# Two images' rows first: the end of a mixture-of-experts layer in another order, on one core of Trainium2

## The chip, the core and the metric

The kernel runs on one core of a Trainium2 chip. The metric is the device time of one execution in microseconds (us), less is better; "before" and "after" are medians of several executions. The core has five engines that run side by side, each with its own instruction queue: TensorE (PE; its weight loads are PEld), VectorE (DVE), ScalarE (ACT), GpSimd (POOL) and SyncE (SP). Data move between the on-chip memory and DRAM by DMA, which SP, ACT and POOL issue from their queues. An engine runs its queue strictly in order: what stands behind a waiting instruction waits too.

## What is computed

Input are 4 images of 256 channels on 32 x 32 points, so 4 x 1024 tokens. A first layer (a selective scan, convolutions, attention over all tokens of an image, a depthwise convolution) makes `x`. Then follows the part that the change is about, a layer of 8 experts of which each token uses two:

```python
t = tokens(x)                                   # (4, 1024, 256)
xf = layernorm(t).reshape(-1, 256)
top_w, top_i = top_k(xf @ Wg + bg, 2)           # two experts of each token
top_w = softmax(top_w)
for e in range(8):
    h = gelu(xf @ W1[e] + b1[e])                # 256 -> 1024
    out += w_dense[:, e:e+1] * (h @ W2[e] + b2[e])   # 1024 -> 256
x = channels_first(t + out)                     # (4, 256, 32, 32)
```

## The kernel before

**Two parallel streams.** The kernel writes out the order of every engine by hand (`tc.manual_schedule`): generators for the scan, the convolutions, the attention, the routing and the expert tiles each give a few instructions and then a number of ticks to wait, and `beat()` lets whichever is due go on. While the last image is still in the first layer, the expert tiles of earlier images fill TensorE.

**Routing.** When an image is ready, `dispatch` writes its tokens, as rows of 256, to the DRAM table `Y` (the residual `t`), finds the two experts of each, and scatters the normalised rows to the DRAM table `XS`, where every expert has a region of its own, filled in the order of the images. So an expert's first rows belong to images 0 and 1, its last ones to image 3.

**Tiles and series.** The expert products are made in tiles of 256 rows of one expert (in some of 320, the "wide" series, which take a short rest along). Which expert and which rows a tile has is known only on the chip; the program has a fixed number of places for tiles, in four series: `SERIES = (8, 8, 21, 8)`. Series 0 and 1 run on the rows of the images that are already there. Series 2 (called `rest`) and 3 (`wide`) share out all that is left after image 3. Of these the last 9 and the last 4 places are "late": they are rarely needed, and stand behind a branch on the chip (`tc.If(any_late > 0)`). For each series, `table` and its callers `series` and `wide_series` compute with some 20 small DVE instructions which expert each place has and its first row; SP reads these numbers from the chip's memory into registers before it issues the loads of a tile.

**The order of the tiles** is the list `order` in `tiles()`: the 16 of series 0 and 1, then four times one wide tile and three of `rest`, 32 in all. I number them 0 to 31. A tile has these steps, with their lines in the profile:

- `rows` (L2164): SP loads the rows, `xs<-XS`; `load` (L2198 to L2203): SP loads the expert's weights, `w`, 2 MB in four transfers, and its biases, `b`. Both are written out while the tile before runs; weights have two sets of buffers, so a transfer waits until the tile before last is done with its set.
- `front` (L2222 to L2246): TensorE transposes the rows into `xp`, DVE copies them to `xT` and reads each row's weight and destination. It stands in TensorE's order in the middle of the second product of the tile before.
- `tile`: the first product `h<-xT,w` on TensorE (L2263), GELU on ACT to `hs` (L2268), the second product `y<-w,hs` (L2276), the bias on DVE to `ys` (L2290, both blocks of 128 rows at once), the row weights on DVE (L2295), and for each block one indirect DMA that POOL issues and that adds the rows to `Y` (L2303). Adds of one tile wait for the adds of the tile before.

**The end.** After the last tile a few instructions judge whether the sums of the attention's exponentials stayed in range (`any`, `bad`, L1608 and L1609; if not, the whole network would be run again in another form). Then `run` branches over the late tiles, and `bring_back` runs for each of the four images: SP reads the image's rows from `Y` in two transfers of 512 KB (`yy<-Y`, L2319; all eight stand at the head of the work behind the branch), TensorE transposes them (`op`, L2328), DVE and ACT copy them (`o`, L2334 and L2332), and ACT writes each half, 512 KB, to the output (L2335). `o` has two buffers.

**The branch.** Every engine runs it for itself. Where it is not taken, each engine passes a short block that adds to the semaphores what the skipped work would have added; it first waits until the semaphores have reached the count that they have before the branch. SP does this for the eight semaphores of the DMAs that SP and ACT issue, POOL for those of its own DMAs.

Of the kernel before, what the change touches and what calls it, by code (L numbers as in the profile page):

```python
# [14 lines left out]
P = 128  # L15
C = 256
# [32 lines left out]
LATE, LATE_WIDE = 9, 4  # L49

# [25 lines left out]
def network(  # L76
# [71 lines left out]
    with tc.tile_pool(name="w_conv", bufs=1) as wp, tc.tile_pool(  # L148
# [239 lines left out]
        def a8(name):  # L388
            return act8.tile([P, NC2, N], F32, tag="a8", name=name)
# [7 lines left out]
        def a4(name):  # L397
            return act4.tile([P, N], F32, tag="a4", name=name)
# [979 lines left out]

        def tiles():
# [5 lines left out]
            between = (experts.SERIES[rest] - LATE) // some  # L1385
            for i in range(some):
                order.append((wide, i))
                order += [(rest, i * between + k) for k in range(between)]
# [50 lines left out]
            def ahead(n, at):  # L1439

                if experts.placed and wide not in tables:
                    tables[wide] = experts.series(wide, temp)
                    tables[rest] = experts.series(rest, temp)
                if n == len(order):
                    return
                if n in got and len(got[n]) > 4:
                    return
                if n in xs and n in got and at >= 5:
                    front(n)
                    return  # L1450

                if known(n) and n not in tables_of:
                    table(n)
                if n not in xs and sent(n):
                    rows(n)
                if n not in got and known(n):
                    load(n)

            for n in range(len(order)):
# [19 lines left out]
                for at, _ in enumerate(experts.tile(  # L1479
                    n, s, got[n], hs,  # L1480
                    act4.tile([P, len(experts.blocks(s)), C], F32, tag="a4", name=f"ys_{n}"),
                )):
                    if at < 4:
                        loaded[0] = None
                    ahead(n + 1, at)
                    yield T.get(("pace",), 1)
# [54 lines left out]
        with tc.manual_schedule(engines=ALL):  # L1541
# [54 lines left out]
            start(one_by_one(joined(B - 1), around(B - 1), sent_off(B - 1)))  # L1596
            drain()

    if not shifted:
        with tc.tile_pool(name="judge", bufs=1) as jp:  # L1600
            most = jp.tile([P, 1], F32, name="most")
            for i, span in enumerate((SPAN, INVERSE)):
                nc.vector.tensor_scalar(sums[:, i, :], sums[:, i, :], span, None, ALU.is_lt)
            nc.vector.tensor_reduce(most, sums.rearrange("p a b -> p (a b)"), AX.X, ALU.min)

            nc.vector.tensor_scalar(most, most, 1.0, None, ALU.is_lt)
            any_ = ps_tile("any")
            nc.tensor.matmul(any_[0:1, 0:1], ones_mean[:, 0:1], most, start=True, stop=True)  # L1608
            nc.vector.tensor_scalar(bad, any_[0:1, 0:1], 0.0, None, ALU.is_gt)  # L1609

    experts.run(experts.tables)
# [11 lines left out]
class Experts:  # L1623
# [19 lines left out]
    def __init__(self, ctx, tc, psum, B, b1, ident, eps5, ones_mean, Wg, bg, W1, W2, b2, out):  # L1643
# [74 lines left out]
        self.read = []  # L1718
        self.apart = m0.tile([P, 1], F32, name="apart")
# [251 lines left out]
    def count_up(self, s, temp):  # L1971

        nc, K, n = self.nc, self.NTOK // self.T, self.SERIES[s]
        steps = temp(f"steps_{s}", [P, NE, K])
        base = {self.WIDE: 0, self.WIDE - 1: REST}.get(s, self.T - 1)
        nc.gpsimd.iota(
            steps, [[0, NE], [self.T, K]], base=base,
            channel_multiplier=0, allow_small_or_imprecise_dtypes=True,
        )
        which = temp(f"which_{s}", [P, n, NE])  # L1980
        nc.gpsimd.iota(
            which, [[1, n], [0, NE]], base=0, channel_multiplier=0,
            allow_small_or_imprecise_dtypes=True,
        )
        self.numbers[s] = steps, which

# [8 lines left out]
    def table(self, temp, keep, name, n, ntile, which, done=None):  # L1995
# [3 lines left out]
        ends = keep(f"ends_{name}", [P, 1, NE])  # L1999
        nc.vector.tensor_tensor_scan(  # L2000
            ends[:, 0, :], self.every[:, 0:NE], ntile[:, 0, :], 0.0, ALU.mult, ALU.add
        )
        starts = temp(f"starts_{name}", [P, 1, NE])
        nc.vector.tensor_tensor(starts, ends, ntile, ALU.subtract)
        S = [P, n, NE]
# [7 lines left out]
        nc.vector.tensor_scalar(expert, expert, float(NE - 1), None, ALU.min)  # L2013
# [7 lines left out]
        nc.vector.tensor_tensor(which, which, self.region[:, 0:1, :].to_broadcast(S), ALU.add)  # L2021
# [13 lines left out]
    def use(self, s, ends):  # L2035

        late = LATE_WIDE if s == self.WIDE else LATE
        over = self.used[s] = self.m0.tile([P, 1], mybir.dt.int32, name=f"over_{s}")
        self.nc.vector.tensor_scalar(
            over, ends[:, :, NE - 1 : NE].rearrange("p a e -> p (a e)"),  # L2040
            float(late - self.SERIES[s]), 0.0, ALU.add, ALU.max,
        )

    def wide_series(self, temp):
# [34 lines left out]
        self.use(s, ends)  # L2079
        return table  # L2080

    def series(self, s, temp):
# [7 lines left out]
        if s == self.WIDE - 1:  # L2090
            assert before + n == self.NTILE
            table, _, ends = self.table(temp, self.kept, s, n, self.left, which, self.done)
            self.use(s, ends)
            self.any_late = self.m0.tile([P, 1], mybir.dt.int32, name="any_late")
            nc.vector.tensor_tensor(
                self.any_late, self.used[s], self.used[self.WIDE], ALU.add
            )
            return table
# [18 lines left out]
    def run(self, tables):  # L2117

        tc, nc = self.tc, self.nc
        with tc.tile_pool(name="moe2", bufs=2) as m2:  # L2120
            def load(v):
                return nc.values_load(
                    v[0:1, 0:1], min_val=0, max_val=sum(self.SERIES),
                    skip_runtime_bounds_check_because="made from counts of at most NTOK rows",
                )

            def late_tile(s, i):
                j, W = f"{s}_{i}", self.width(s)
                w1 = m2.tile([P, NC2, DFF], F32, tag="w1", name=f"w1_{j}")
                w2 = m2.tile([P, NHC, C], F32, tag="w2", name=f"w2_{j}")  # L2130
                got = self.load(
                    s, i, tables[s], [w1], [w2], m2.tile([P, C], F32, tag="b2", name=f"b2_{j}")
                )
                xs = m2.tile([P, len(self.blocks(s)), self.ROW], F32, tag="xs", name=f"xs_{j}")
                self.rows(s, i, tables[s], xs)
                got += self.front(
                    j, s, i, tables[s], xs, m2.tile([P, NC2, W], F32, tag="xT", name=f"xT_{j}")
                )
                for _ in self.tile(
                    j, s, got, [m2.tile([P, NHC, W], F32, tag="hs", name=f"hs_{j}")],  # L2140
                    m2.tile([P, len(self.blocks(s)), C], F32, tag="ys", name=f"ys_{j}"),
                ):
                    pass

            with tc.If(load(self.any_late) > 0):
                for s, late in ((self.WIDE - 1, LATE), (self.WIDE, LATE_WIDE)):
                    n = self.SERIES[s]
                    with tc.If(load(self.used[s]) > 0):
                        for i in range(n - late, n):
                            late_tile(s, i)  # L2150
            for b in range(self.B):
                self.bring_back(b, m2)
# [96 lines left out]
    def tile(self, j, s, got, hs, ys):  # L2249
# [9 lines left out]
        for k0 in range(0, NHC, each):  # L2259
# [9 lines left out]
            if k0 % 2 == 0:  # L2269
                yield  # L2270
        for t, n in blocks:
            if t % 2 == 0:
# [9 lines left out]
            if parts > 1:  # L2282
# [3 lines left out]
                nc.vector.tensor_tensor(ys[0:n, t], yp[0:n, 0:C], other, ALU.add)  # L2286
            elif t % 2 or t == len(blocks) - 1:
# [6 lines left out]
        for t, n in blocks:  # L2294
            nc.vector.tensor_scalar(  # L2295
                ys[0:n, t, :], ys[0:n, t, :], wgt[0:n, t, :], None, ALU.mult
            )

        added = []
        for t, n in blocks:  # L2300
            if t:
                nc.gpsimd.memset(self.apart, 0.0)
            ins = nc.gpsimd.indirect_dma_start(  # L2303
                out=self.Y[:, :],
                out_offset=bass.IndirectOffsetOnAxis(ap=dest[0:n, t, :], axis=0),
                in_=ys[0:n, t, :], in_offset=None, compute_op=ALU.add,
            )
            for other in added:
                self.tc.declare_no_dep(ins.ins, other.ins, reason="no two share a row")
            self.follow(ins, self.added, "a row may be added to by both")  # L2310
            added.append(ins)
        self.added = added

    def bring_back(self, b, m2):

        nc, NT = self.nc, self.NT
        y = m2.tile([P, NT, C], F32, tag="yy", name=f"yy_{b}", bufs=self.B)
        for h in range(2):
            nc.sync.dma_start(  # L2319
# [3 lines left out]
        o = m2.tile([P, NC2, N], F32, tag="o", name=f"o_{b}")  # L2323
# [112 lines left out]
```

## Time and profile before

| | us |
|---|---|
| median of 3 runs | 2177.85 (2172.67 to 2179.22) |
| the profiled execution | 2175.2 |
| its span, first to last instruction | 2173.3 |
| TensorE busy | 1937.3 (89% of the span) |
| DVE busy | 1536.4 (71%) |
| ACT busy | 1211.4 (56%) |
| POOL busy | 1042.7 (48%) |
| granted TensorE clock, mean | 0.956 |
| data moved by DMA | 251.41 MB, 116 GB/s in the mean |

The profile is of one execution. Lines of the timeline give the start and the length in us, the engine, the line of the program, the operation with its tiles as output<-input, its shape, and in brackets how long the engine had been idle and what released it. SPq, ACTq and POOLq are the queues of these engines: a row DMA_DIRECT2D there is the issue of a transfer, not its duration. Lines of a source query give the count and the shortest, median and longest duration in ns, and the first and last start in us. The tables by stage give for each engine its busy time and the number of its instructions, then the granted clock of TensorE (1.00 is full speed), the busy share of the 16 DMA engines and what they moved.

### The profile page before, as it was taken

The page shows a single profiled execution, that of the slowest core. Times are in us where ns is not written, and L with a number is a line of the kernel's source. Part 1 is how long each engine was busy: PE and PEld are TensorE (multiplying, and loading weights), DVE is VectorE, ACT ScalarE, POOL GpSimd, SP SyncE. Part 2 cuts the span into 40 slices and gives each one's busy share as a digit, 9 for nine tenths or more (in the row PEclk, how much of TensorE's full clock was granted, in tenths as well). Part 3 has the DMA queues.
Part 4 walks back from the last instruction along what each step waited for, and adds up shares of the span by engine and source line. Part 5 has one row for each costly group of instructions (what it writes and reads, how often), then busy time and mean ns, then how long its engine had stood idle before and what let it go on. Part 6 is the DMA issues. An engine that isn't in the chain of part 4 may idle for free. (4 is left out here: it accounts for less than half of the span.)

```text
span 2173.3 us, 28179 instructions
## 1 busy us (share of the span) xinstructions
PE 1937.3 (89%) x8690; PEld 867.6 (40%) x8690; DVE 1536.4 (71%) x2231; ACT 1211.4 (56%) x2272; POOL 1042.7 (48%) x930
## 2 busy tenths in 40 slices
PE   6778778999987999988789999679999999999995
PEld 2112112322212332222124223126743668888884
DVE  4989999957998989699898998985364445121111
ACT  4665657668777577776566876524277423222221
POOL 0887887712788850476887026742021113322221
PEclk8888999999999999998999999889999999999997
DMA  3565553401444431154634204344330267866665
GB/s 104 148 156 131 127 123 93 100 28 57 104 117 114 105 73 40 29 138 104 168 81 118 69 22 107 85 164 139 92 82 21 55 189 215 255 182 187 178 159 167
DMA packets 157088, 251.41 MB, mean 116 GB/s; under 512 B 34740, under 2 KB 101332, under 8 KB 156664
## 3 DMA queue, kind: packets, MB, share of 16 engines
q1 hardware_dynamic: 136560, 223.47, 37.6%
q0 software_dynamic: 12720, 17.32, 4.1%
q10 hardware_dynamic: 7640, 8.65, 1.2%
q8 instruction: 72, 1.18, 0.2%
q14 instruction: 96, 0.79, 0.1%
HBM read 137.22 MB, written 36.62 MB: 80 GB/s over the span
## 5 line engine op out<-in xcount | busy, mean ns | idle before, releaser
L744 POOL TENSOR_TENSOR dA<-hs,cs 128x512 f32<-128x512 f32 x512 | 682.0, 1340 | 376.1 <-DVE hs L736 307.6
L715 ACT ACTIVATE dA<-dts,A 128x512 f32<-128x512 f32 x512 | 358.9, 718 | 160.9 <-DMA dts<-dt 66.7
L754 PE MATMUL yp<-dA,quads 128*32 128x512 f32 x1024 | 289.0, 637 | 87.8 <-POOL dA L744 76.0
L2303 POOL DMA_INDIRECT Y<-ys,dest x68 | 109.5, 1610 | 429.6 <-DVE ys L2295 422.5
L1133 ACT ACTIVATE e<-st 128x512 f32<-128x512 f32 x512 | 263.8, 606 | 89.4 <-PE st L1123 88.9
L2268 ACT ACTIVATE hs<-h,b 128x256 f32<-128x256 f32 (+1 forms) x256 | 110.0, 478 | 345.7 <-PE h L2263 233.8
L725 DVE TENSOR_TENSOR dBu<-dts,bs 128x512 f32<-128x512 f32 x384 | 259.6, 677 | 47.4 <-PE bs L707 13.4
L736 DVE TENSOR_TENSOR_SCAN hs<-dA,last,dBu 128x512 f32<-128x512 f32 x192 | 243.6, 1269 | 1.8 <-PE yp L754 1.1
L2276 PE MATMUL y<-w,hs 128*128 128x256 f32 (+1 forms) x1088 | 242.6, 382 | 0.5 <-ACT hs L2268 0.3
L2263 PE MATMUL h<-xT,w 128*128 128x256 f32 (+1 forms) x1024 | 239.6, 390 | 1.1 <-DVE xT L2226 1.1
L736 DVE TENSOR_TENSOR_SCAN hs<-dA,dBu 128x512 f32<-128x512 f32 x192 | 231.6, 1206 | 1.0 <-PE var L435 0.7
L1180 DVE TENSOR_TENSOR e<-e,e 128x512 f32<-128x512 f32 x256 | 168.2, 718 | 77.8 <-ACT e L1133 47.8
L2263 PEld LDWEIGHTS h<-xT,w 128*128 128x128 f32 x1024 | 195.2, 192 | 42.8 <-issue 8.6
L2276 PEld LDWEIGHTS y<-w,hs 128*128 128x128 f32 (+1 forms) x1088 | 197.1, 188 | 37.7 <-issue 10.1
L2226 DVE COPY xT<-xp 128x512 f32<-128x512 f32 (+1 forms) x36 | 23.3, 646 | 250.9 <-PE xp L2222 245.1
L707 PE MATMUL bs<-u,xpwT_s 128*32 128x512 f32 x1024 | 161.2, 660 | 41.3 <-DVE hs L736 18.0
L1123 PE MATMUL st<-qk 32*128 32x512 f32 x1024 | 174.0, 638 | 0.3
L754 PEld LDWEIGHTS yp<-dA,quads 128*32 128x32 f32 x1024 | 50.5, 113 | 303.4 <-POOL dA L744 198.6
L1172 PE MATMUL av<-e,v 128*32 128x512 f32 x1024 | 139.5, 604 | 0.0
L1936 POOL DMA_INDIRECT XS<-XR,to x64 | 65.4, 1021 | 90.3 <-ACT e L1133 53.9
L1123 PEld LDWEIGHTS st<-qk 32*128 32x128 f32 x1024 | 59.5, 183 | 115.3 <-issue 85.6
L1144 PE MATMUL av<-e,every 128*32 128x512 f32 x512 | 85.2, 596 | 2.7 <-DVE e L1180 2.6
(335 smaller groups left out, 2639.1 us busy)
## 6 DMA issues: line engine op xcount, KB each, us to landing
dts<-dt SPq DMA_DIRECT2D x512, 128.0 KB
w<-in_W_dram SPq DMA_DIRECT2D x124, 512.0 KB
cs<-cd SPq DMA_DIRECT2D x512, 64.0 KB
xs<-XS SPq DMA_DIRECT2D x32, 260.0 KB
xd<-xn SPq DMA_DIRECT2D x64, 128.0 KB
xn<-in_x_dram SPq DMA_DIRECT2D x8, 512.0 KB
XL<-xl SPq DMA_DIRECT2D x8, 512.0 KB
xl<-XL SPq DMA_DIRECT2D x4, 1024.0 KB
```

The costliest lines, as they stand in the source:

```text
L707: nc.tensor.matmul(bs[r], xpwT_s[:, n, s : s + 1].to_broadcast([P, 32]), T[b, n, "u"][:, half(h)], start=True, stop=True,)
L715: nc.scalar.activation(dA, T[b, n, h, "dts", g][:, 0, :], AF.Exp, scale=A[:, g, n, q : q + 1])
L725: nc.vector.tensor_tensor(dBu, T[b, n, h, "dts", g][:, 1, :], T[b, n, h, "bs", q], ALU.mult)
L736: nc.vector.tensor_tensor_scan(hs, T[b, n, h, "dA", i], dBu, 0.0 if h == 0 else last, ALU.mult, ALU.add)
L744: nc.gpsimd.tensor_tensor(dA, hs, T[b, n, h, "cs", q], ALU.mult)
L754: nc.tensor.matmul(T[b, n, h, "yp"][ts(g, 32)], quads, T[b, n, h, "dA", q * GD + g], start=False, stop=(q == GS - 1),)
L1123: nc.tensor.matmul(sts[i], k[r, ts(kt, P)], q[r, half(h)], start=True, stop=not shifted)
L1133: ins = nc.scalar.activation(es[i], sts[i], AF.Exp, scale=1.0 / HD**0.5)
L1172: nc.tensor.matmul(accs[0][ts(i, HD)], v8[:, kt, ts(4 * g + i, HD)], es[i], start=(kt == 0), stop=(kt == NK - 1),)
L1180: nc.vector.tensor_tensor(first[i], first[i], es[i], ALU.add)
L2263: nc.tensor.matmul(hp[:, i, :], w1(c, k0 + i), xT[:, c, :], start=(c == 0), stop=(c == NC2 - 1))
L2276: nc.tensor.matmul(yp[ts(k % parts, n), ts(t % 2, C)], hidden(k)[:, ds(t * P, n)], w2(k), start=(k < parts), stop=(k >= NHC - parts),)
```

## The change

In the order of the tiles, the first wide tile is followed by eight tiles of `rest` (`EARLY = 8`), then by one more, and then wide ones and `rest` ones alternate: W, 8 R, R, W, R, W, R, W, R. The table of `rest` is sorted anew: places go first to those tiles of each expert that still hold rows of images 0 and 1 (`SOON = 2`), expert by expert, then to the others, so it is computed for 16 kinds instead of 8. It is computed when the first wide tile runs; before, both tables were computed as soon as image 3 had been placed. Should the tiles with rows of images 0 and 1 be more than eight, or should a wide tile hold such rows, `redo` is set and these two images are read and turned once more in the branch.

`bring_back` is split into `fetch` (the reads) and `turn` (transposes, copies, writes). The reads of images 0 and 1 are written out in tile 26, the first tile behind the nine of `rest`; they are turned directly behind the last tile, ahead of the branch. Images 2 and 3 are read and turned behind it. The last tile has its two blocks of rows in two banks, and adds the first block's rows while the second block's product runs. The judging of the sums is a generator of its own that runs while later tiles do. The late tiles use the pools of the main part instead of a pool of their own.

```diff
+EARLY, SOON = 8, 2
...
             some = experts.SERIES[wide] - LATE_WIDE
-            between = (experts.SERIES[rest] - LATE) // some
+            order += [(wide, 0)] + [(rest, i) for i in range(EARLY)]
+            final = len(order)
+            between = (experts.SERIES[rest] - LATE - EARLY) // some
             for i in range(some):
-                order.append((wide, i))
-                order += [(rest, i * between + k) for k in range(between)]
+                order += [(wide, i)] * (i > 0)
+                order += [(rest, EARLY + i * between + k) for k in range(between)]
...
                 if experts.placed and wide not in tables:
                     tables[wide] = experts.series(wide, temp)
+                if wide in tables and rest not in tables and order[n - 1] == (wide, 0):
                     tables[rest] = experts.series(rest, temp)
...
                     ahead(n + 1, at)
+                    if n == final + 1 and at == 4:
+                        for b in range(SOON):
+                            experts.fetch(b, a8(f"yy_{b}"))
                     yield T.get(("pace",), 1)
...
             start(one_by_one(joined(B - 1), around(B - 1), sent_off(B - 1)))
+            if not shifted:
+                start(judged())
             drain()
-    if not shifted:
...
-    experts.run(experts.tables)
+            for b in range(SOON):
+                experts.turn(b, a8(f"o_{b}"))
+
+        experts.run(experts.tables, a8, a4, a2)
...
+            first, second = both[:, :, 0:NE], both[:, :, NE : 2 * NE]
+            nc.vector.tensor_tensor(first, self.soon, self.done, ALU.subtract)
+            nc.vector.tensor_scalar(first, first, 0.0, None, ALU.max)
+            nc.vector.tensor_tensor(first, first, self.left, ALU.min)
+            nc.vector.tensor_tensor(second, self.left, first, ALU.subtract)
...
+            table, _, ends = self.table(temp, self.kept, s, n, both, which, done, 2 * NE)
...
+            with tc.If(load(self.redo) > 0):
+                for b in range(SOON):
+                    self.fetch(b, a8(f"yy_{b}_again"))
+                    self.turn(b, a8(f"o_{b}_again"))
+        for b in range(SOON, self.B):
+            self.fetch(b, a8(f"yy_{b}"))
+        for b in range(SOON, self.B):
+            self.turn(b, a8(f"o_{b}"))
...
+            elif apart:
+                nc.vector.tensor_tensor(ys[:, t], yp[:, ts(t % 2, C)], b2_s, ALU.add)
+                weigh(t, n)
+                add(t, n)
```

## The prediction

> **What bounds the kernel now.** I read the page's busy shares first, then busy time by stages, then the timeline of the end, then the two places that the change touches earlier. The page's chain of waits names only the last 0.6%, so the end is followed by the timeline instead. By stages (engine columns PE, PEld, DVE, ACT, POOL, then granted clock, DMA share, GB/s):
>
> ```profile
> 1870.00:2135.00 265.00, 265.00 (x1251) 222.27 (x1249) 50.39 (x168) 62.17 (x141) 61.78 (x59) 1.00 0.63 170
> 2135.00:2174.00 39.00, 12.06 (x68) 10.34 (x66) 6.68 (x12) 4.68 (x8) 3.23 (x3) 0.64 0.68 226
> ```
>
> From 1870 to 2135 TensorE is never idle: it alone sets when the last product ends, and DMA has 37% of its time free. After it come 38 us in which TensorE works 12. That end, line by line:
>
> ```profile
> 2128.15 7.07 PE L2276 MATMUL y<-w,hs 128*128 128x256 f32 x32
> ...
> 2138.47 1.56 POOL L2303 DMA_INDIRECT Y<-ys,dest  x1 [0.19 <-POOLq L2145]
> 2143.75 7.93 SPq L2319 DMA_DIRECT2D yy<-Y  x8
> ...
> 2148.49 4.75 PE L2328 MATMUL op<-ident,yy 128*128 128x128 f32 x24 [13.16 <-DMA yy<-Y]
> ...
> 2151.13 0.45 ACTq L2335 DMA_DIRECT2D out_dram<-o  x1
> ...
> 2165.91 0.38 ACTq L2335 DMA_DIRECT2D out_dram<-o  x1
> ```
>
> Call X the end of the last product, 2128.15 + 7.07 = 2135.22. The last add is issued at X + 3.25, the eight reads of Y start at X + 8.5, the last write is issued at X + 30.7, the span ends at X + 38.1. Between the last add and the reads lies the branch's skipped side:
>
> ```profile
> L2145 POOLq EVENT_SEMAPHORE  x6: 17/30/43, 2138.3 to 2142.3; - x6
> ...
> L2145 POOLq INC_SWDGE_SEM  x1: 986/986/986, 2142.4 to 2142.4; - x1
> ```
>
> So the add has landed by 2142.3 (3.8 us after its issue), POOL needs 0.99 us more, then SP may read. From there DMA is the limit: 4.19 MB are read and 4.19 MB written, and the DMA view of this window shows 350 to 400 GB/s nearly throughout. A 512 KB transfer takes about 1.4 us at 370 GB/s.
>
> **The change, part by part.**
>
> *Order of tiles, and the inputs.* I took the routing from the reference on the given inputs. Before the last series experts 0 to 5 have had 3, 3, 2, 3, 3, 2 tiles; 12 normal and 4 wide tiles are left, as many as are laid out; 6 tiles (at most 8 fit) still hold rows of images 0 and 1, and no wide one does. So neither the late tiles nor the repeat run. The same 32 tiles run, 14.3 us for a normal and 18.1 us for a wide one in this stage, in another order: 0.
>
> *Judging the sums.* A one-column product (2 records, 0.19 us at 2135.15) and a compare of 0.13 us leave the end; they land in tile 5, near 1730, where TensorE has gaps (44.8 of 50 us busy). +0.1 on the path.
>
> *Table of the last series.* Before, it is built right behind the wide one, ahead of tile 13's copy. Afterwards it is built when the first wide tile (tile 16) has begun, twice as wide, and SP can't load tile 17's rows and weights before it is there:
>
> ```profile
> 1840.61 0.16 DVE L2000 TENSOR_TENSOR_SCAN ends<-every,left 128x8 f32<-128x8 f32 x1
> ...
> 1844.36 0.18 DVE L2027 TENSOR_SCALAR table<-first 128x21 int32<-128x21 f32 x1
> ...
> 1845.45 7.17 PE L2263 MATMUL h<-xT,w 128*128 128x256 f32 x32 [0.28 <-DVE xT L2226]
> ...
> 1891.00 0.62 DVE L2295 TENSOR_SCALAR ys<-ys,wgt 128x256 f32<-128x256 f32 x2
> ...
> 1902.14 0.60 PE L2222 MATMUL xp<-ident,xs 128*128 128x128 f32 x4
> ```
>
> First the gain: the 3.9 us of DVE at 1840.6 shrink to eight small operations (some 1.8 us), and TensorE's 0.28 us behind them go: -0.3. Then the cost: in DVE's order the new table stands behind tile 15's weighing, over at 1891.62. It is the old chain of 3.9 us, plus 0.17 us for each of nine operations on 336 instead of 168 columns, one more region add (0.4), and eight small ones (0.2 each): about 7.9 us, so 1899.5. SP takes 0.65 us to the issue of the next rows (in SP's timeline: b's issue over at 1910.2, xs at 1910.85), a transfer's data begin 1.2 us after issue, 260 KB take 0.7, and landing is known 1.3 us after the last byte (in the DMA view the last write's data are through at about 2169.8, the wait for it is over at 2171.2). Rows are there at 1903.4 to 1904; TensorE wants them at 1901.93, when the first weight load for this transpose starts (SP had issued them at 1877.91). In between nothing else is queued for it, so it waits 1.7 us. Bounds: 0 if the table is quicker, 4 if DVE's dependent steps or SP are slower; 1.7 is built from rows nearest to it. Weights follow the rows: 2 MB issued by 1904 land by 1910 for products at 1909.7 (w1 first, by 1907): covered. POOL's wider iotas (0.98 us for 168 columns at 1798.7) lie where POOL is 3/4 idle.
>
> *Reading images 0 and 1 beside later tiles.* Four 512 KB reads stand on SP behind tile 27's loads and ahead of tile 28's. They wait for tile 25's adds, about 7 us into tile 26 (an add is issued 3.3 us after a tile's end and lands 3.8 later). While SP waits, tile 28's rows and weights stand behind it: SP is past at 11 us and data at 15 us into tile 26; the rows are needed at 18.1 + 10.8 = 29 us and the weights at 32. Slack of 12 us: cost 0, as DMA is 37% free. Tile 26's adds must wait until the reads are over, but are not ready before 19 us. Without this cover every further us of SP's wait would be one of TensorE's.
>
> *The last tile in two halves.* The second half's sum (0.42 as for 64x256, half of 0.69 else) and weighing (0.31) precede one add, issued at X + 0.95 instead of X + 3.25. Alone it would let the reads start at X + 6.2.
>
> *Turning images 0 and 1 behind the last product.* 32 transposes at 0.133 (8 in 1.06) are 4.3 us of an idle TensorE. Writes are issued at X + 1.75, 2.9, 4.0, 5.0; data begin 1 us after the first, 4 x 1.4 us: X + 8.4, known at X + 9.7.
>
> *The new wait.* SP's skipped side of the branch waits for all eight hardware-DMA semaphores to reach their counts before it adds to them. Before, no such transfer was open there. In the built order of the changed kernel the four writes of images 0 and 1 count up four of these. So SP can't read images 2 and 3 at X + 6.2, but at about F = X + 10.0. Queued behind it: all four remaining reads, hence everything.
>
> *Reads, turning and writing of images 2 and 3.* Data F + 1.7 (2143.75 to 2145.4) to F + 7.4; the last half is known at F + 8.7; its turning and copies take 2.7 (2148.46 to 2151.13): write issued F + 11.4. ACT issues the second write behind a copy of the next image, so four writes end at F + 14.5, known 15.8, end 2.1 later: F + 17.9.
>
> Here the clock weighs against the change. The row: in this end TensorE ran 24 transposes in 4.75 us (0.198 each), cold at first and then faster. [...] The turning is now two bursts with 10 us between. If all of the second stayed cold, a half would take 2.1 us against an arrival each 1.4, and the last write would be issued 2.4 us later. By the row it keeps up; I take the row, and keep 2.4 for the range.
>
> **The sum.** X moves by +0.1 - 0.3 + 1.7 = +1.5. The end moves from X + 38.1 to X + 27.9: -10.2. Together -8.7 us, on the profiled execution's 2175.2 us (span 2173.3): 2166.5. The median of the three runs, 2177.85, lies 2.65 above that execution; with the same difference 2169.1.
>
> **The rivals.**
> *A: the writes don't hold the reads.* Then F = X + 6.2 and reads overlap the first writes; some 0.5 us is lost to sharing: X + 24.6, with X + 1.5: -12, 2165.9. For it: semaphores may have been met by then if writes are quick. Against: four writes can't be done before X + 8.
> *B: the same, but dearer.* Table stall 4, cold transposes 2.4, or writes beside the adds at 300 GB/s (+1.3 on F): -3 to -6, within what counts as no change; about 2173.
> *C: slower.* SP's wait in front of the reads of Y, in tile 26, starves tiles 28 and later. Price: 1 us of TensorE per us beyond 12 us of slack; it must exceed 12 + 8.7 = 21 us to cost more than the end gains, and 27 us to be seen; at 30 us the result is about 2187. Against: tile 25's adds are the only thing waited for, and adds landed within 4 us of issue here.
> *D: the change doesn't do what it says*, since a tile too many makes the branch be taken and images 0 and 1 be read and turned again: by the counts above (6 of 8) it isn't; it would add some 20 us. Counted with C.
>
> **Chances.** Forecast 60%, A 15%, B 20%, C with D 5%. A measurement of this kernel can tell about 0.3% (6.5 us) from no change; the forecast's gain is 8.7, so with runs that differ by 6 us some of it falls inside. Faster by over 0.3%: 0.85 x 60 + 15 + 0.2 x 20 = 70%; within: 9 + 16 = 25%; slower 5%. Range 2163 to 2174.5: from A less 3 us of scatter to B's dear end.
>
> **What would show it.** Tile 17's rows are issued on SP near 1900 and TensorE idles 1 to 3 us before that transpose. Reads of Y appear inside tile 26 with TensorE still full to the end. After X: an ACT write within 2 us, the first read of images 2 and 3 about 10 us after X and just behind the fourth write's landing, the end 28 us after X. I am wrong if the reads begin 6 us after X (A), if TensorE is idle in tiles 27 to 29 (C), or if line groups of late tiles appear (D).

## The result and the profile after

The median goes from 2176.07 us (12 executions, 2171.6 to 2180.85) to 2168.16 us (12 executions, 2163.2 to 2174.57): ratio 0.9967, 95% interval 0.9957 to 0.9978, so 4.8 to 9.4 us less. 2169.1 was forecast. The profiled execution after the change took 2167.03 us with a span of 2165.3.

The stages again, with the same columns as before the change (engines, granted clock, DMA share, GB/s), cut at the end of the last product:

```profile
1870.00:2136.50 266.50, 266.50 (x1257) 223.41 (x1256) 58.17 (x199) 61.92 (x140) 63.55 (x61) 1.00 0.65 178
2136.50:2166.00 29.50, 9.34 (x65) 8.83 (x63) 6.12 (x10) 4.68 (x8) 1.57 (x1) 0.77 0.68 228
```

TensorE is still never idle up to the last product; the stretch behind it is 29 us instead of 38. The timeline of the changed end:

```profile
2129.59 7.07 PE L2365 MATMUL y<-w,hs 128*128 128x256 f32 x32
...
2136.49 3.66 PE L2412 MATMUL op<-ident,yy 128*128 128x128 f32 x32
2137.79 1.57 POOL L2350 DMA_INDIRECT Y<-ys,dest  x1 [1.77 <-DVE ys L2343]
2138.24 0.39 ACTq L2419 DMA_DIRECT2D out_dram<-o  x1
...
2141.36 0.61 ACTq L2419 DMA_DIRECT2D out_dram<-o  x1
2147.55 2.08 SPq L2399 DMA_DIRECT2D yy<-Y  x4
2151.49 5.69 PE L2412 MATMUL op<-ident,yy 128*128 128x128 f32 x32 [11.34 <-DMA yy<-Y]
2152.67 0.69 DVE L2418 COPY o<-op 128x512 f32<-128x512 f32 x1 [12.23 <-PE op L2412]
...
2157.99 0.38 ACTq L2419 DMA_DIRECT2D out_dram<-o  x1
```

X is now 2129.59 + 7.07 = 2136.66. Images 0 and 1 are turned at once, their four writes are issued at X + 1.6 to X + 4.7, and SP starts the four remaining reads at F = X + 10.9. The last write is issued at X + 21.3, the span ends at X + 28.6. Why F is so late stands on the line of the branch (count, shortest, median and longest ns, first and last start):

```profile
L2208 POOLq EVENT_SEMAPHORE  x6: 17/30/43, 2138.6 to 2144.0; - x6
L2208 SPq EVENT_SEMAPHORE  x4: 17/17/17, 2141.7 to 2147.2; - x4
...
L2208 PEldq COMPARE_BRANCH  x1: 4871/4871/4871, 2138.6 to 2138.6; - x1
...
L2208 POOLq INC_SWDGE_SEM  x1: 986/986/986, 2144.1 to 2144.1; - x1
```

POOL is through with the last add at 2144.1 + 0.99 = 2145.1; SP's skipped side only gets through its semaphores at 2147.2, and 0.35 us later come the reads. The four rows of SPq are its waits for the four writes. The trace's DMA records have the bulk of the writes' data until 2145.9 (X + 9.2) and their last packets until 2146.9.

Images 0 and 1 are read in tile 26, which begins at 2038.56 (issues in SP's queue):

```profile
2045.91 2.03 SPq L2399 DMA_DIRECT2D yy<-Y  x4
...
2048.57 0.38 SPq L2233 DMA_DIRECT2D xs<-XS  x1
```

SP is past them 10 us into the tile. At the wait for the new table, TensorE's weight load is held by 0.41 us, while its products run on without a gap:

```profile
1899.64 0.18 DVE L2061 TENSOR_SCALAR table<-first 128x21 int32<-128x21 f32 x1
...
1900.77 0.39 SPq L2233 DMA_DIRECT2D xs<-XS  x1
...
1903.51 0.42 PEld L2291 LDWEIGHTS xp<-ident,xs 128*128 128x128 f32 x4 [0.41 <-DMA xs<-XS]
```

### The profile page after: what moved, and what is told of

Read it like the earlier page. It is cut to its first block, busy times and chain, and to the rows that moved or that the text cites. A ratio compares the mean times of both kernels' runs of the same rounds, so it can differ in the third digit from the quotient of the medians.

```text
span 2165.3 us, 28187 instructions
## 1 busy us (share of the span) xinstructions
PE 1931.0 (89%) x8690; PEld 867.6 (40%) x8690; DVE 1540.5 (71%) x2252; ACT 1212.3 (56%) x2272; POOL 1043.4 (48%) x931
## 5 line engine op out<-in xcount | busy, mean ns | idle before, releaser
L728 DVE TENSOR_TENSOR dBu<-dts,bs 128x512 f32<-128x512 f32 x384 | 259.6, 677 | 46.0 <-PE bs L710 10.8
L710 PE MATMUL bs<-u,xpwT_s 128*32 128x512 f32 x1024 | 162.9, 669 | 40.3 <-DVE hs L739 17.3
```

Source lines behind the costliest of these rows:

```text
L710: nc.tensor.matmul(bs[r], xpwT_s[:, n, s : s + 1].to_broadcast([P, 32]), T[b, n, "u"][:, half(h)], start=True, stop=True,)
L728: nc.vector.tensor_tensor(dBu, T[b, n, h, "dts", g][:, 1, :], T[b, n, h, "bs", q], ALU.mult)
```

## The experiments

My theory was the one on record: the early reads and the early turning shorten the end, and the price is that SP's skipped side of the branch waits for the early writes. The main rival was A: these writes hold nothing. All numbers of the end are counted from X, since X itself drifts (second experiment). F and the end are read in the one profile of each kernel (of the kernel before there are two). The measured ends, in us:

| kernel | F - X | end - F | end - X |
|---|---|---|---|
| before | 8.5 | 29.6 | 38.1 |
| before, profiled again | 8.7 | 30.2 | 38.8 |
| halves of the last tile alone | 6.4 | 30.0 | 36.4 |
| four output buffers alone | 8.6 | 28.1 | 36.6 |
| changed, no early reads | 6.1 | 27.4 | 33.6 |
| changed, turned behind the branch | 6.3 | 22.7 | 29.0 |
| changed | 10.9 | 17.7 | 28.6 |
| changed, early writes left out | 7.0 | 19.8 | 26.8 |
| changed, two early writes | 8.5 | 21.1 | 29.5 |
| changed, last tile undivided | 12.8 | 18.5 | 31.3 |
| changed, TensorE kept busy | 10.8 | 18.0 | 28.8 |
| changed, all ahead of the branch | 6.5 | 23.9 | 30.4 |
| changed, reads in tile 26 four times | 11.2 | 18.2 | 29.3 |
| changed, slow table | 10.9 | 17.3 | 28.2 |

The last two rows change something ahead of the end and nothing in it. So the same end came at X + 28.2, X + 28.6 and X + 29.3 in three profiles: where two rows differ by about 1 us or less, no effect is shown.

**Do the early writes hold the reads?**

```diff
-                experts.turn(b, a8(f"o_{b}"))
+                experts.turn(b, a8(f"o_{b}"), False)
...
-            nc.scalar.dma_start(
+            if write:
+                nc.scalar.dma_start(
```

> The changed kernel without the four early writes: images 0 and 1 are read and turned as there, but not written, so these two images of the output are left out. X is the end of the last product, F the start of the reads of images 2 and 3; the changed kernel had F = X + 10.9 and its span ended at X + 28.6. My theory (SP's skipped side of the branch waits for the landing of those writes): the add is issued at X + 1.1, lands 3.8 later as in the kernel before, POOL needs 1.0, so F = X + 6.2 and the end about F + 17.8 = X + 24. Rival 1 (the writes hold nothing, SP needs that time anyway): F stays at X + 10.9. Rival 2 (the add itself takes 6.2 us to land in this place, whether writes run or not): F = X + 8.5.

F fell to X + 7.0. What SP waited for shows it directly (engine and line, releaser, us in total, times, longest). The changed kernel:

```profile
SPq L2208 <- SPq L2208: 36.3, 4, 30.7
```

These are the four waits for the writes; the longest began some 25 us before X, when SP had nothing else left to do. The same view without the early writes:

```profile
SPq L2399 <- DMA Y<-ys,dest: 32.4, 2, 31.3
```

With the writes, SP stands in the branch's block (L2208); without them it is past the block and the reads wait for the add, as they did before the change. Rival A falls. POOL's line tells how the 3.9 us are made up:

```profile
L2208 POOLq INC_SWDGE_SEM  x1: 986/986/986, 2149.0 to 2149.0; - x1
```

Here X is 2143.12, so POOL is through with the add at X + 6.8; in the changed kernel it was at X + 8.4, as the add landed later beside the writes. So of the 3.9 us some 1.6 are the add that the writes slow down, and the other 2.3 are SP's own wait for the writes. The end gained less than F: X + 26.8, not X + 24. In this run all transposes of the second burst came every 0.213 us, and the data of the four reads took about 8 us instead of 7; I did not separate these two.

**How much does a profile drift?** The kernel before, unchanged.

> The kernel before, profiled once more, as a control on how much the profiles of one kernel differ. Between the two profiles shown, tile 0 began 2.5 us later after the change than before it, and X came 1.4 us later. If executions of one kernel drift by that much (theory: the 1.4 us are mostly drift), the start of tile 0 and X of this profile differ from the first one of the kernel before by 1 to 3 us. If the changed program causes it (rival), both agree within 0.3 us.

Tile 0 began 3.4 us earlier and X came 4.2 us earlier than in the first profile. Over all 14 profiles tile 0 begins between 1445.9 and 1460.1. So X can't be compared between two profiles. The steps from tile 15 on can; of those before, some differ by 3 us between these two (tile 8 took 26.3 and 23.0). From the start of tile 16 to that of 17 it took 17.93 us in all four profiles with the old table, 18.13 to 18.36 in nine of the changed order.

**Do the halves of the last tile buy anything?** First taken out of the changed kernel:

```diff
-                    n == len(order) - 1,
+                    False,
```

> The changed kernel with the last tile as the other tiles, both blocks in one bank and added at the end. The two adds are then issued up to X + 3.25, as in the kernel before. My theory (the early writes decide F): F stays within 0.5 us of X + 10.9, since the writes land at X + 10.5 and the adds, 6.2 us after issue and 1.0 for POOL, at about the same time; the halves bought nothing here. Rival (the adds decide): F = X + 10.9 + 2.2 = X + 13.1 and the end at X + 30.8.

The expectation fell: F is X + 12.8, near the rival's X + 13.1, but not by the rival's path, in which the adds decide:

```profile
L2208 SPq EVENT_SEMAPHORE  x9: 17/17/17, 2111.8 to 2149.8; - x9
L2208 POOLq INC_SWDGE_SEM  x1: 986/986/986, 2147.6 to 2147.6; - x1
```

X is 2137.34: POOL was through with the adds at X + 11.2, SP with its block only at X + 12.5, so the writes decided. They were issued 0.5 us later than in the changed kernel (from X + 2.1 on), and the two adds, issued at X + 1.4 and X + 3.3, now move their data amid them: the DMA records show the bulk of the writes spread over 8.3 us instead of 7. The halves help by taking most of the adds' data out of the writes' way. Then put alone into the kernel before:

> The kernel before with one part of the change alone: the last tile has its two blocks in two banks and adds the first while the second is made. Theory: F goes from X + 8.5 and 8.7 (two profiles of the kernel before) to X + 6.1, as in the run of the order alone, and the end follows: X + 35.7 to 36.3 instead of X + 38.1 and 38.8. Rival (the time from F on grows, since something else is late, as the turning or the bank): end above X + 37.

F = X + 6.4, end X + 36.4: 1.7 to 2.4 us gained, a shade above the expected range.

**What is left without any early read?** The order, the table, the halves and the judging stay, the "order alone" of the expectations:

```diff
-                    if n == final + 1 and at == 4:
-                        for b in range(SOON):
-                            experts.fetch(b, a8(f"yy_{b}"))
...
-            for b in range(SOON):
-                experts.turn(b, a8(f"o_{b}"))
...
-        for b in range(SOON, self.B):
+        for b in range(self.B):
             self.fetch(b, a8(f"yy_{b}"))
-        for b in range(SOON, self.B):
+        for b in range(self.B):
             self.turn(b, a8(f"o_{b}"))
```

> The changed order, table, halves and judging alone: no image is read or turned before the branch, all four behind it. Theory: without early writes F is set by the one add of the last half, as in the run without writes (X + 7.0), and from F the end takes what it took in the kernel before (F + 29.6 there): X + 36.6, so 8 us later than the changed kernel's X + 28.6, and 1.5 to 2 us better than before's X + 38.1. Rival (most of the gain is in the order or the halves, not in the early reads): X + 33 or less.

```profile
2127.99 7.07 PE L2356 MATMUL y<-w,hs 128*128 128x256 f32 x32
...
2141.18 7.33 SPq L2390 DMA_DIRECT2D yy<-Y  x8
```

The span was 2168.6. It ended at X + 33.6, close to the rival: from F on it took 27.4 us, not 29.6. A cause offers itself in the second profile of the kernel before (the first one has the same wait, of 5.3 us):

```profile
2156.39 0.59 ACT L2332 COPY o<-op 128x512 f32<-128x512 f32 x1 [5.22 <-DMA out_dram<-o]
```

The copies of image 2 wait 5.2 us until a write of image 0 has landed: two output buffers for four images. The change takes these buffers from a pool of eight. Tried in the kernel before:

```diff
-        o = m2.tile([P, NC2, N], F32, tag="o", name=f"o_{b}")
+        o = m2.tile([P, NC2, N], F32, tag="o", name=f"o_{b}", bufs=self.B)
```

> The kernel before with four buffers for the turned images instead of two. The run of the order alone took 27.4 us from F to the end, the kernel before 29.6 and 30.2, with the same reads, turning and writes behind the branch. Theory (in the kernel before the copies of image 2 wait until the writes of image 0 have landed; the change takes this wait away by taking its buffers from the larger pool): F stays at X + 8.6, from F to the end it takes 27 to 27.8. Rival (the buffers don't matter, the reads are spread otherwise): F + 29.5 to 30.2.

From F to the end: 28.1 us, 1.5 to 2.1 less, though not quite the expected 27 to 27.8. This wait is a part of what the kernel before loses that I had not named. In the changed kernel two buffers should have done as well, though no run tries it: its first copy of image 2 starts at 2152.67, 5.5 us after SP has found all early writes landed (2147.2).

**Early reads or early turning?** Images 0 and 1 are read in tile 26 into the space of first-layer weights that are no longer used, but turned behind the branch.

```diff
-                            experts.fetch(b, a8(f"yy_{b}"))
+                            experts.fetch(b, parted(b))
...
-            for b in range(SOON):
-                experts.turn(b, a8(f"o_{b}"))
...
-        for b in range(SOON, self.B):
+        for b in range(self.B):
             self.turn(b, a8(f"o_{b}"))
```

> The changed kernel with images 0 and 1 read early, but turned and written behind the branch, ahead of images 2 and 3. It separates the early reads from the early turning. Theory: no writes are open at the branch, so F is about X + 6.5 as without writes; TensorE passes its block (4.9 us) by X + 7 and turns cold, so writes are issued from X + 8.5 on; twelve transfers of 1.42 us from X + 8 and what follows the last one (3.8) end at X + 28.5 to 29.5: within 1 us of the changed kernel, so most of the gain is in the reads. Rival (the early writes are the gain): X + 31 or later, near the X + 33.6 without early reads.

```profile
2127.38 7.07 PE L2366 MATMUL y<-w,hs 128*128 128x256 f32 x32
...
2140.75 2.08 SPq L2407 DMA_DIRECT2D yy<-Y  x4
```

With a span of 2163.4 this is X + 29.0, as expected. The early reads are worth 4.6 us (33.6 to 29.0). The early turning and writing have 0.4 left, less than the same end differs by between profiles, so no gain of theirs is shown: what the writes gain by starting at X + 1.6, the wait for them takes back.

**What does SP's wait in tile 26 cost when it grows?** The reads in tile 26 with `times = 4`:

```diff
-        for h in range(2):
+        for h in list(range(2)) * times:
```

> The changed kernel with the early reads of images 0 and 1 in tile 26 made four times (16 transfers, 8.4 MB instead of 2.1). It prices the wait in front of the loads of tile 28. My theory (12 us of slack, then 1 us of TensorE per us): SP is past the reads 6 us later and their data are through 17 us later at 370 GB/s, so rows of tile 28 land about 33 us into tile 26 and are wanted at 29: TensorE is idle 4 to 5 us in front of tile 28 and X moves by as much. Rival (the loads of tile 28 don't queue behind the data of the reads, or the slack is larger): no idle time, X as in the changed kernel within 0.5 us counted from the start of tile 26.

The 4 to 5 us were far off, since a repeated read into the same place waits for the one before it. The first line is of SP's waits (us in total, times, longest): twelve, one for each repetition.

```profile
SPq L2399 <- DMA yy<-Y: 23.8, 12, 4.6
...
2038.93 30.78 SPq L2399 DMA_DIRECT2D yy<-Y  x16
...
2070.27 0.38 SPq L2233 DMA_DIRECT2D xs<-XS  x1
...
2075.41 1.87 PE L2291 MATMUL xp<-ident,xs 128*128 128x128 f32 x6 [15.16 <-DMA xs<-XS]
```

This makes it a test of the price at another size. Tile 26 starts at 2031.69 here, so SP issues tile 28's rows 38.6 us into it, 28.6 later than in the changed kernel; TensorE was idle for 15.2. If each us beyond the slack is one of TensorE's, which one size of wait can't show, the slack was 28.6 - 15.2 = 13.4 us (12 was forecast). But tile 28 came 18.0 us later, 2.8 more than TensorE idled.

**Is the table the last arrival at tile 17?**

```diff
-            nc.vector.tensor_scalar(first, first, 0.0, None, ALU.max)
+            for _ in range(21):
+                nc.vector.tensor_scalar(first, first, 0.0, None, ALU.max)
```

> The changed kernel with 20 idle repetitions of one of the small operations that the table of the last series is made of. It takes 3 to 4 us more of DVE in that chain. In five profiles with the table at tile 16 the step from the start of tile 16 to that of tile 17 was 18.15 to 18.37 us against 17.93 in both profiles of the kernel before. Theory (the rows of tile 17 are the last arrival, just 0.2 to 0.4 us late, and every further us of the table is one of TensorE's): the step becomes 21.3 to 22.3 us. Rival (those 0.2 to 0.4 us come from elsewhere, the table has some us in hand): the step stays below 19.5.

The step became 25.2 us. The 20 operations took 4.9 us (0.246 each with their gaps, not 0.15 to 0.2), and TensorE, which had not idled in front of this transpose in the changed kernel, idled as long:

```profile
1906.72 1.11 PE L2292 MATMUL xp<-ident,xs 128*128 128x128 f32 x4 [4.94 <-DMA xs<-XS]
1907.63 7.22 PE L2366 MATMUL y<-w,hs 128*128 128x256 f32 x32
```

The theory holds 1 to 1; the other 2.2 us are in these two rows, 0.66 and 5.50 us long in the changed kernel. By stages (granted clock third from the end):

```profile
1906.70:1911.00 4.30, 4.28 (x12) 3.58 (x13) 1.24 (x5) 0.00 (x0) 0.00 (x0) 0.50 0.95 355
1911.50:1915.50 4.00, 4.00 (x26) 2.69 (x25) 0.87 (x2) 0.37 (x1) 0.00 (x0) 1.00 0.99 307
```

After the idle stretch TensorE is granted half its clock for some 4 us. The run before shows the same behind its 15.2 us, and the extra 2.8 us go with it:

```profile
2075.40:2079.50 4.10, 4.09 (x11) 2.76 (x12) 2.40 (x10) 0.00 (x0) 3.72 (x5) 0.50 0.92 303
```

**Does the cold clock cost the end anything?** In the changed kernel the second burst of transposes starts cold, that is at a granted clock of 0.50:

```profile
2151.50:2155.50 4.00, 4.00 (x19) 3.94 (x20) 1.38 (x2) 0.91 (x2) 0.00 (x0) 0.50 1.00 349
```

So TensorE was given 26 transposes without use ahead of it.

```diff
+        warm = self.psum.tile([P, HALF], F32, tag="ps", name="warm")
+        for t in range(26):
+            nc.tensor.transpose(warm[:, ts(t % 4, P)], self.ident, self.ident)
         for b in range(SOON, self.B):
             self.turn(b, a8(f"o_{b}"))
```

> The changed kernel with 26 idle transposes on TensorE behind the branch, before those of images 2 and 3, so that it isn't idle for the 11 us between the two bursts. In the changed kernel the first 19 transposes of the second burst came every 0.213 us and the others every 0.11 us. Theory (the clock is halved after the idle time and costs the end about 1 us: writes of 304, 208 and 222 KB in three successive us where DMA does 370): the second burst runs at 0.11 us from its first or second transpose, its four groups wait for data instead, and the end comes 0.7 to 1.2 us nearer to F than F + 17.75. Rival (the data set the pace anyway): transposes are quick but the end stays at F + 17.5 to 17.8.

```profile
2159.30:2165.50 6.20, 4.33 (x32) 3.42 (x32) 2.46 (x4) 1.76 (x3) 0.00 (x0) 1.00 0.88 306
```

The whole second burst ran at the full clock, and the end was at F + 18.0, within the 17.3 to 18.2 of the three profiles without these transposes: the rival. The transposes waited for the reads instead. In this end the data set the pace.

**Can the wait be taken away?** Once by doing everything ahead of the branch, with a repetition inside it:

```diff
+            for b in range(SOON, B):
+                experts.fetch(b, a8(f"yy_{b}"))
-            for b in range(SOON):
+            for b in range(B):
                 experts.turn(b, a8(f"o_{b}"))
...
-            with tc.If(load(self.redo) > 0):
-                for b in range(SOON):
-                    self.fetch(b, a8(f"yy_{b}_again"))
-                    self.turn(b, a8(f"o_{b}_again"))
+            for b in range(self.B):
+                self.fetch(b, a8(f"yy_{b}_again"))
+                self.turn(b, a8(f"o_{b}_again"))
```

> All four images are read and turned ahead of the branch; inside it, behind the late tiles, all four are read and turned once more (this path is not taken here). SP then waits for the adds alone, not for the writes of images 0 and 1. In the changed kernel the last add had landed at X + 7.4, and the reads began at X + 10.9. Theory: F = X + 7.5 to 8, the last write is issued 10.4 after F and known 15 to 16 after F, at X + 23.5. But both branches now stand behind everything: TensorE is through with turning at X + 17 and passes two branch blocks of 4.8 us each (4871 and 4749 ns in the changed kernel), so the span ends at X + 27 to 27.5, only 1 to 1.5 us earlier than the X + 28.6 of the changed kernel. Rival 1: the blocks are covered by the writes, end at X + 25 (3.5 us gained). Rival 2: the SP block adds its own wait behind the last write [...]: X + 29 or later, nothing gained.

```profile
2144.16 3.16 SPq L2396 DMA_DIRECT2D yy<-Y  x4
```

X is 2137.66, so F was X + 6.5. The four writes are open here as in the changed kernel, and only the branch no longer stands between the add and the reads: this is the plainest sign that the block's wait holds the reads, and not the writes' traffic alone (POOL's 1.0 us goes away with it). Yet the end was X + 30.4, as the second rival had it, 1.8 later than in the changed kernel (ratio to before 0.9973, interval 0.9963 to 0.9983). Both branch lines in SP's queue, the late tiles' and that of the whole network:

```profile
L2210 SPq EVENT_SEMAPHORE  x9: 17/17/17, 2153.4 to 2161.4; - x9
```

```profile
L74 SPq EVENT_SEMAPHORE  x9: 17/17/17, 2164.7 to 2165.3; - x9
```

SP passes the first block at 2161.4, 3.9 us after the last write was issued (2157.54), and then the second 4 us later: two blocks in a row stand open at the end, where the changed kernel hides one of them under its waits. And once by writing only image 0 early; image 1 is turned ahead of the branch, into two buffers of its own (`turned`), and written behind it:

```diff
+        for h in range(2):
+            self.write(1, h, self.turned[h])
         for b in range(SOON, self.B):
             self.turn(b, a8(f"o_{b}"))
```

> The changed kernel with only image 0 written ahead of the branch: image 1 is turned there too, into buffers of its own, but its two writes stand behind the branch on ACT, ahead of the work on images 2 and 3. Theory (the count of open writes sets F, then the volume sets the end): the two writes have landed by about X + 6.7, so the add decides with about X + 7.3, 3.6 us earlier than in the changed kernel; but 10 transfers of 512 KB instead of 8 then follow, 2.8 us more, so the span ends at X + 27.3 to 28, a gain of 0.6 to 1.3 us that the medians can't tell from the changed kernel's. Rival 1 (F alone sets the end): X + 25. Rival 2 (F isn't set by the writes' count but by the four writes' data): F stays above X + 9.

The expectation fell: F was X + 8.5, not X + 7.3 (the add took 6.1 us to land beside the two writes, then POOL's 1.0), and the two held writes shared the DMA with the reads: end X + 29.5, 0.9 later than in the changed kernel, no more than the same end differs by. Its ratio to before, 0.9951 (0.9933 to 0.9968, four executions), overlaps that of the changed kernel. No version tried is shown to be better than the changed kernel.

## Why the prediction was right

**The end from X on.** Forecast 38.1 to 27.9, measured 38.1 to 28.6. From F on the forecast was 17.9 and 17.7 came, in part by luck: the last write was issued at F + 10.4, not F + 11.4, but from there it took 7.3 us to the end, not 6.5 (7.4 in the kernel before, 2165.91 to 2173.3). F was forecast at X + 10.0 and came at X + 10.9. The step that failed in size is "data begin 1 us after the first, 4 x 1.4 us: X + 8.4": the writes were issued a little earlier than forecast, and their data began about 0.9 us after the first issue (2138.24 to some 2139.1), but the add's 128 KB were moved in between (in the microsecond from 2141 the DMA records have 0.09 MB of the add and only 0.11 MB of the writes). The bulk was through 0.8 us later, the last packets nearly another 1 us after it. Rival B had this as "writes beside the adds", +1.3 on F. The undivided last tile shows the same in large. The 1.3 us between the last byte and its being known are mostly such a thin rest of data, in the kernel before too: its last packets of the writes came at 2170.8, and SP's wait was over at 2171.2. And the DMA view of the kernel before, read as 350 to 400 GB/s nearly throughout, has nine of its 31 busy slices below 350, down to 180: the wait for output buffers falls into this stretch, so that data were not its limit all along.

**The new wait** was the right mechanism: without the writes F falls by 3.9 us (X + 10.9 to X + 7.0), and SP's wait changes its place; with the writes but without the branch in between F was X + 6.5. Of the eight semaphores of the forecast, four made SP wait at this branch (36.3 us in sum); at the branch of the whole network SP waited eight times in the second profile of the kernel before (L71: 19.5 us in sum, the longest 5.7). I had put nothing at the add's later landing beside the writes, which is some 1.6 of the 3.9 us. What I had not seen is that the wait eats the gain of the early writing: 0.4 us are left of it, too little to be told from none. The sum did not need that, since it followed the end as a whole, and for the same reason it held the buffers' 1.5 to 2 us without naming them: it had all writes of images 2 and 3 wait for turning only.

**X.** Forecast +1.5; between the two profiles shown it came +1.44, and that agreement is luck. The steps: the table stall, forecast 1.7, is 0.2 to 0.4 us in nine profiles. The term was mis-sized: the chain of DVE took 7.1 us (1892.74 to 1899.82), not 7.9, SP issued the rows 0.95 us after it, not 0.65, and they landed 2.75 us after their issue, not 3.2 or more. The 1.2 us from issue to data in that sum are what the reads of Y took in the kernel before: the first is issued at 2143.75, its first data show at about 2144.95. The relief at tile 13, forecast -0.3, is -0.45 (14.70 to 14.25), and 0.1 more came on the next tile. Judging, forecast +0.1, is +0.3 on tile 5 (33.40 to 33.71). So these edits leave X where it was within a few tenths, and the forecast's -8.7 should have been about -9.5, with some 1 us of scatter in the ends. The interval of the medians, -4.8 to -9.4, ends about there. Tile 0 starts at 1449.7 in the mean of the four profiles with the old order and at 1452.0 in that of the ten with the new one, but single ones scatter over 14 us; so it stays open whether something ahead of tile 0 takes a part back. That the forecast of 2169.1 lies within 1 us of the median is then partly luck: X was put 1.5 us too late, and the medians differ by less than the measured steps of X and of the end would make.

**Early reads:** no idle time of TensorE in tiles 27 to 31, as forecast, with a slack of about 13.4 us instead of 12. Neither the late tiles nor a repetition ran (D): both pages count 8690 products of TensorE. Rival C's price was too low in one respect: the two idle stretches that the runs made, 4.94 us at tile 17 and 15.2 us at tile 28, cost another 2.2 and 2.8 us, which go with the halved clock behind them.

**The clock.** The forecast's 2.1 us for a half that stays cold, and the 2.4 us with it, were an estimate. In the end of the kernel before the granted clock was 0.50 over the first 4.0 us of the turning (2148.5 to 2152.5) and 1.00 behind them, and eight transposes took 1.06 us at 1.00: twice that is 2.1. At 0.50 they came every 0.213 us in the changed kernel, which makes 1.7 for a half. The changed kernel and the one with the slow table had the low clock in these places: 0.50 for 4.0 us behind 11.3 us of idling at the end, and 0.50 for 4.3 us behind 4.94 us at tile 17. Within the idle stretch the clock fell after 3.5 us in the end before the change (at 2138.8) and after 5.2 us in the end after it (at 2145.4). I had taken the row, by which the turning keeps up, and kept 2.4 us for the range; keeping TensorE busy gained nothing, so the row was right here. There was reason for the reserve, though: without the early writes all 32 transposes came every 0.213 us, as the first 19 do at 0.50 in the changed kernel (the mean granted clock from 2150 to 2164 was 0.54), and the end was at F + 19.8, but as the reads were slower there too, the clock's share is not shown.

## What to carry to other kernels

Before you move transfers ahead of a branch, look at what its skipped side waits for: here the four open writes of ACT's queue became a wait for what stands behind the branch (the reads began at X + 10.9, and at X + 7.0 without these writes), and early writes gave back what they gained, as far as these profiles can tell, while early reads, which were over by then, kept their gain. Follow a tail in absolute times from one anchor, take that anchor's drift from a second profile of the unchanged kernel before you explain its shift, and take the scatter of the tail from profiles in which it is the same. When a part of the gain has no step in your list, look for what came along with the edit, such as a pool with more buffers.

## What was not expected of the hardware

- An add by indirect DMA landed 3.8 us after its issue in the kernel before and 4.7 in the run without early writes, but 6.2 beside four writes and 6.1 beside two.
- The branch instruction holds TensorE for long, 4871 ns at L2208 and 4749 ns at L74 in the changed kernel (3591 ns at L2145 and 4169 ns at L71 in the kernel before), against 45 to 72 ns on POOL, DVE, ACT and SP. The row of the first branch stands among the lines of L2208 above. No run here shows what these microseconds are spent on.
- An idle stretch of 4.94 us in front of one tile cost 7.1 us in all, 2.2 of it beside a granted clock of 0.50 in the 4.3 us behind it.
